# A second level of seven products for the graph layer's weights, and the residual and both biases added by accumulating DMAs

## The chip, the cores and the metric

The kernel runs on one NeuronCore of a Trainium2 chip. The metric is the device time in microseconds of one execution, the median of three runs. Profiles come from a separate profiled execution, whose own time is given beside its span.

## The reference

Two graph layers on x of shape 32 x 512 x 512 (batch, node, feature) in fp32, with one 512 x 512 adjacency matrix. Cut to what matters:

```
q, k, v = x @ Wq + bq, x @ Wk + bk, x @ Wv + bv            # 8 heads of 64
weights = softmax(q k^T / 8 + (adj == 0 ? -1e9 : 0))       # over the neighbours j
x1      = layernorm(x + weights @ v)                        # per node, over 512 features
deg     = adj.sum(1);  A = adj * deg^-1/2 (rows) * deg^-1/2 (columns)
out     = layernorm(x1 + A @ (x1 @ W1) + b1)
```

Each row of the softmax weights sums to one, so the bias of v may be added to the attention's output instead of to v.

## The kernel before

Everything is done per batch element, in fp32, and the engines overlap the work of several batches. `stretch` (two heads pairs at a time, `ORDER[:2]` and then `ORDER[2:]`) computes the scores, masks them on VectorE, takes the exponential on ScalarE, sums the numerators on GpSimd (`accumulate`), and multiplies by v. A batch b has two stretches. Between the first and the second stand the key and query projections of batch b + 1; after the second stand, in one list of pieces that `play` walks through, the convolution of batch b - 1 and the values of batch b + 1. The text calls this last list the second half of b. TensorE therefore repeats: scores and value products, projections, scores and value products, second half.

Projections are not plain products. Both 512-long dimensions are cut in two, and `seven` forms the four blocks of a result from seven products instead of eight, with sums of input blocks prepared beforehand (`combine` for x, `weigh_part` for weights; slots 4 to 6 hold sums, slot 2 is overwritten). A table such as `CHAIN` lists for each product its PSUM region (A, B, D), the two slots, and where its running sum goes: `put` writes a block, `add` adds to one. A region keeps accumulating over its products, so the next product on a region has to wait until the last one's running sum has been read out. The values of batches 1 and up use a second level: the four products of `CHAIN` that the table `OUTER` doesn't list are themselves one 2 x 2 block product, and `LEAF` does it by seven products of quarter size (four matmuls of 128 x 128 by 128 columns each) with quarter sums of x (`quarter`, `QUARTERS`) and of Wv (`weigh_quarters`, `wv_quarters`). A half-size product is four matmuls with 256 columns. One matmul in fp32 stands in the trace as two records.

The convolution of batch b - 1 comes in two factors. The first (`first`) multiplies the normalised x1, split in a high and a low part (`hi`, `lo`), by the transposed adjacency, and ScalarE copies the result into a tile `zT`. The second (`second`) multiplies it by W1 with the seven half-size products of `CHAIN`; each running sum goes through `move` on VectorE, and `put` adds x1 with b1 (in `yT`) on the way, so that the tile `y` holds the sum. After that come statistics, normalisation and the store.

What sets the order: TensorE, VectorE, ScalarE and GpSimd run in the order in which the program calls them (`InOrder`); `play(main, beside)` walks through `main`, which calls TensorE, and after piece n calls what `beside[n]` lists for the other engines. Waits between engines are semaphores, put in by the framework from the tiles' uses. Transfers issued on SyncE may be placed by the scheduler. [...]

Lines the change touches, by their function: the bias of v is added on GpSimd by `bias_values`, four adds of 128 x 512 per batch; the residual x is loaded by `load_residual` into a tile `xr` (four transfers of 256 KB on SyncE) and added to `yT` on GpSimd by `add` in `finish`; b1 is added on GpSimd by `lift`. `yT` is the attention's output after a transposition by VectorE and DMAs of 128-byte runs (`unload_values`), scaled by the softmax's inverse sums on VectorE (`scale`). `NUM` is a tile of eight numerators of 128 x 1024, taken in rotation by `numerators()`; each stretch takes exactly eight. `load_x` loads the next x in two halves, one into a tile of its own, the other into slot 7 of `NUM`. `wqv` holds either the query or the value weights; `swap` reloads it from DRAM twice a batch.

Of the kernel before, what the change touches and what calls it, by code (L numbers as in the profile page):

```python
# [18 lines left out]
P = 128  # L19
# [31 lines left out]
def unshifted(  # L51
# [61 lines left out]
    X = {}  # L113
# [9 lines left out]
    def load_x(b, j):  # L123
        if j == 1:
            X[b, j] = NUM[:, 7].rearrange("p k (n t r) -> p (k n) t r", t=DT, r=32)
        else:
            X[b, j] = acts.tile([P, 8, DT, 32], F32, name="x", bufs=1)
        for q in range(4):
            nc.sync.dma_start(
                X[b, j][32 * q : 32 * (q + 1)],  # L130
                x[b, ts(j, HALF), ts(q, P)].rearrange("(k s) (t r) -> s k t r", s=32, r=32),
            )
# [51 lines left out]
    def load_residual(b):  # L184
        if b < LAST - 1:
            t = acts.tile([P, NT, D], F32, name="xr", tag="zT", bufs=1)
        else:
            t = wk[:, 3:].rearrange("p k u o -> p k (u o)")
        R[b] = [t[:, i, :] for i in range(NT)]
        for i in range(NT):  # L190
            nc.sync.dma_start(R[b][i], x[b, ts(i, P), :])

# [33 lines left out]
    R[0] = acts.tile([P, NT, D], F32, name="xr", tag="zT", bufs=1)  # L226
    R[0] = [R[0][:, i, :] for i in range(NT)]

    wv = NUM[:, :4].rearrange("p e k (u o) -> p (e k) u o", u=2)
    for i in range(2):  # L230
        for k, engine in enumerate((nc.sync, nc.scalar)):
            engine.dma_start(R[0][2 * i + k], x[0, ts(2 * i + k, P), :])
            load_parts(Wv, "wv", engine, wv, [(i, 2 * k), (i, 2 * k + 1)])
        if i == 0:
            bv_r = load_row(bv, "bv_r", nc.scalar)
# [14 lines left out]
    stored = [drams.tile([P, 7, 2, HALF], F32, name=f"{name}_parts") for name in ("wq", "wv")]  # L250

    def weigh_quarters(engine):
        old, new = wv[:, 1:5].rearrange("p k u (r o) -> p k u r o", r=2), wv_quarters
        engine.tensor_tensor(new[:, 0], old[:, :, 0, 1], old[:, :, 1, 1], ALU.add)
        engine.tensor_tensor(new[:, 1], new[:, 0], old[:, :, 0, 0], ALU.subtract)
        engine.tensor_tensor(new[:, 2], old[:, :, 0, 0], old[:, :, 0, 1], ALU.subtract)
        engine.tensor_tensor(old[:, :, 0, 1], old[:, :, 1, 0], new[:, 1], ALU.subtract)
# [49 lines left out]
    def degrees():  # L307
# [37 lines left out]
    LEAF = tuple(CHAIN[k] for k in (0, 1, 3, 2, 5, 4, 6))  # L345
    OUTER = (
        ("A", (0, 0), (("add", (0, 0)),)),
# [4 lines left out]
    def seven(table, multiply, put, add, shape=(2, HALF)):  # L352
        regions = {}

        def step(region, ij, moves):
            fresh = region not in regions
            if fresh:
                regions[region] = bank([P, *shape])
            p = regions[region]
            multiply(p, *ij, fresh)  # L360
            for kind, q in moves:
                (put if kind == "put" else add)(q, p)

        return each(step, *table)
# [7 lines left out]
    def values_of(b):  # L372
# [10 lines left out]
        def multiply_quarters(p, i, j, fresh):  # L383
            for n, (k, l) in enumerate(((1, 1), (3, 2), (2, 3), (4, 4))):
                right = w[:, k, i % 2, ts(i // 2, P)] if i < 4 else wv_quarters[:, i - 4, k - 1]
                left = XT[:, l, j % 2, ts(j // 2, P)] if j in (0, 1, 3) else QUARTERS[:, max(j - 3, 0), l - 1]
                tensor.matmul(p[:, n, :], left, right, start=fresh and n == 0, stop=True, skip_group_check=True)

        def quarter_of(r, t):
            v = V[b].rearrange("p (j t) (i r o) -> p t r j i o", t=2, i=2, r=2)  # L390
            return v[:, t, r]

        def put_quarters(q, p):
            out(0, 0)
            scalar.copy(quarter_of(*q), p.rearrange("p (j i) o -> p j i o", i=2))

        def add_quarters(q, p):
            to = quarter_of(*q)
            vector.tensor_add(to, to, p.rearrange("p (j i) o -> p j i o", i=2))

        def spread_last():
            gpsimd.tensor_add(out(0, 1), out(0, 1), out(1, 1))

# [13 lines left out]
        leaf = seven(LEAF, multiply_quarters, put_quarters, add_quarters, (4, P))  # L417
        return leaf + [spread_last] + seven(OUTER, multiply, put, add)

    def bias_values(b, n, engine=gpsimd):  # L420
        engine.tensor_add(V[b][:, n, :], V[b][:, n, :], bv_r)
# [152 lines left out]
    def finish(b):  # L574
# [95 lines left out]
        def grow(i):  # L670
# [3 lines left out]
        all_, behind = range(NT), (NT - 1, *range(NT - 1))  # L674
        return dict(
            sums0=[lambda: sums(b, 0, bank([P, N]))], inverse0=[lambda: inverse(0, bank([P, N]))],
# [11 lines left out]
    def convolve(b):  # L688
        t = {}
        last = b == LAST  # L690
# [18 lines left out]
        def take(d, p, copy):  # L709
            if d == 0:  # L710
                t["z"] = XT[:, :4] if last else acts.tile([P, 4, 2, HALF], F32, name="zT", bufs=1)
# [7 lines left out]
        def combine(at):  # L719
            if at == 0:  # L720
                if last:
                    t["parts"] = XT[:, 4:]
                elif b == LAST - 2:
                    t["parts"] = wk[:, :3]
                else:
                    t["parts"] = acts.tile([P, 3, 2, HALF], F32, name="parts", tag="hi", bufs=1)
            to, a, c = PARTS[at]
            engine = vector if last and at < 2 else gpsimd
            engine.tensor_tensor(slot(to), slot(a), slot(c), ALU.subtract)

# [5 lines left out]

        def multiply(p, i, j, fresh):
            if "y" not in t:
                if last:
                    t["y"] = [numerators() for _ in range(2)]  # L740
                else:
                    if b == LAST - 2:
                        y = XT[:, 7:].rearrange("p k u o -> p k (u o)")
                    else:
                        y = acts.tile([P, NT, D], F32, name="y", tag="lo", bufs=1)
                    t["y"] = [y[:, 2 * k : 2 * k + 2, :] for k in range(2)]
# [7 lines left out]
        aside, extend = b == LAST - 1, []  # L754

# [34 lines left out]
        def store(n, at):  # L790
# [12 lines left out]
            parts=each(combine, *range(4)),  # L803
# [24 lines left out]
    weigh_quarters(gpsimd)  # L828
    nc.sync.dma_start(stored[1], NUM[:, :4].rearrange("p e k (u o) -> p (e k) u o", u=2)[:, :7])
    nc.sync.dma_start(stored[0], wqv)  # L830
    run(each(bias_values, *((0, n) for n in range(NT))))
# [6 lines left out]
    quarters()  # L838
# [4 lines left out]
    for b in range(B):  # L843
# [3 lines left out]
        if 1 < b < LAST:  # L847
            load_residual(b - 1)
        if b + 2 < B:
            load_x(b + 2, 0)  # L850
        if b == LAST:
            load_residual(b)
        stretch(b, one, back["measure"][:3] if back else ())
# [12 lines left out]
        if b < LAST:  # L866
            k0, k1 = keys_and_queries(b + 1, 0), keys_and_queries(b + 1, 1)
            main = [p for pair in zip(k0, k1) for p in pair]
            if b == 0:
# [4 lines left out]
                    7: weights[2:3], 8: exact[2:3], 9: weights[3:], 10: exact[3:],  # L874
                }
            else:
# [3 lines left out]
                    0: rest + scale + ahead["add"], 1: store[:1] + fold0, 2: store[1:2], 3: store[2:3] + fold1,  # L880
                    4: store[3:] + measure[:2], 5: measure[2:] + ahead["root"] + [quarters], 7: norm[:1] + ahead["judge"],
                    8: norm[1:2] + low[:1], 9: norm[2:3] + low[1:2], 10: norm[3:] + low[2:3],
                    11: low[3:] + ahead["lift"],
                }
            play(main, beside)
        else:
# [5 lines left out]
                3: conv["parts"][1:] + e["inverse0"] + ahead["grow"],  # L892
            })

        if b < LAST:
            swap(1)
        stretch(b, two, f[b]["pairs"][0] + f[b]["pairs"][1] if b == LAST else ())
# [3 lines left out]
        if b + 2 < B:  # L901
            load_x(b + 2, 1)
        if b < LAST:
            end = f[b]
            v, bias_v = values_of(b + 1), each(bias_values, *((b + 1, n) for n in range(NT)))
            back_to_queries = [lambda: swap(0)] if b < LAST - 1 else []
            if b == 0:
                play(v, {
                    1: fold0, 5: fold1, 8: turn0, 9: turn1 + combined[:2], 10: bias_v + combined[2:] + back_to_queries,
                })  # L910
            else:
                conv = c[b - 1]
                second = conv["second"]
                k = 6 if b < LAST - 1 else 8
                main = conv["first"] + v[:k] + second[:1] + v[k:9] + second[1:2] + v[9:10] + second[2:3] + v[10:] + second[3:]
                grow, parts, scale = ahead["grow"], conv["parts"], end["scale"]
                if b < LAST - 1:
                    beside = {
                        1: parts[:1] + fold0, 3: parts[1:], 5: fold1, 6: grow[:1], 7: end["inverse"], 8: grow[1:2],
                        9: grow[2:3] + scale[:1], 10: grow[3:] + scale[1:2], 11: scale[2:3], 13: turn0, 14: scale[3:],  # L920
                        15: turn1 + combined[:2], 17: combined[2:] + back_to_queries + bias_v,
                    }
                else:
                    measure, norm, low = end["measure"], end["norm"], end["low"]
                    beside = {
                        0: [lambda: load_residual(LAST - 1)], 1: parts[:1] + fold0, 3: parts[1:], 5: fold1,
                        6: grow[:1], 7: end["inverse"], 8: grow[1:2] + scale[3:], 9: grow[2:3] + scale[:1], 10: grow[3:] + scale[1:3] + end["add"],
                        14: measure[:2], 15: measure[2:3], 16: measure[3:] + end["root"],
                        17: norm[:1] + bias_v, 18: norm[1:2] + low[:1], 19: norm[2:3] + low[1:2],
                        20: norm[3:] + low[2:3], 21: low[3:] + end["lift"],  # L930
# [314 lines left out]
```

## Time and profile before

| | |
|---|---|
| median of three runs | 2732.93 us (2732.28 to 2732.99) |
| profiled execution, its own time | 2731.85 us |
| its span | 2730.0 us |
| granted TensorE clock | 0.998 |
| one batch, from TensorE's timeline | 83.78 us |
| of it, the second half from its first value product | 23.84 us |

The page's names are those of tiles with numbers left out: `w` is W1's tile (`w1`), `e` is `NUM`, `mm`, `sc` and `av` are PSUM tiles, `v`, `y`, `yT`, `zT`, `parts` and `xT` are as in the code. Nearly every instruction has line 45, that of `InOrder`, so groups are told apart by tiles. A timeline line gives start, length, engine, operation, output and inputs, how many instructions were merged, and in brackets the idle time before it with what ended it.

### The profile page before, as it was taken

To read this page: it belongs to the slowest core of one execution; us is meant where nothing else is said; L and a number is where in the kernel's file an instruction comes from. 1 tells how busy PE (TensorE), PEld (TensorE's weight loads), DVE (VectorE), ACT (ScalarE), POOL (GpSimd) and SP (SyncE) were. 2 spreads that over 40 slices of the span, in tenths; PEclk is the share of its full clock that TensorE was granted. 3 is DMA by queue.
4 is the path that set the end of the run, shared out by engine and by line. 5 is a ranking of instruction groups with operands and counts; after the bars stand their busy time and mean duration, and the time that the engine had idled before them with its cause. 6 is when DMAs were issued, how large, how long until landed. Compare 5 with 4: busy or idle time off the path is not lost.

```text
span 2730.0 us, 36290 instructions
## 1 busy us (share of the span) xinstructions
PE 2700.8 (99%) x13284; PEld 1907.7 (70%) x13284; DVE 2023.7 (74%) x2809; ACT 1260.5 (46%) x1807; POOL 2026.7 (74%) x1335
## 2 busy tenths in 40 slices
PE   9999999999999999999999999999999999999997
PEld 6676676766767767767667677677676676766765
DVE  4777776777777778767777777777777776777777
ACT  3335444454444454444544445444445444454444
POOL 5778777778777787777777777877778777778775
PEclk9999999999999999999999999999999999999999
DMA  6222333323333233333232332333333333323321
GB/s 181 86 74 88 101 89 99 107 69 105 93 105 97 76 103 104 89 97 97 82 104 86 103 106 73 101 107 90 94 90 92 101 89 98 107 70 104 98 61 45
DMA packets 388186, 256.75 MB, mean 94 GB/s; under 512 B 278816, under 2 KB 346400, under 8 KB 379936
## 3 DMA queue, kind: packets, MB, share of 16 engines
q1 hardware_dynamic: 386848, 252.78, 30.8%
q8 instruction: 107, 1.75, 0.3%
q10 hardware_dynamic: 1152, 1.57, 0.2%
q14 instruction: 79, 0.65, 0.1%
HBM read 183.77 MB, written 37.22 MB: 81 GB/s over the span
## 4 chain that ended last, share of the span: by engine, by line
PE 97%; DVE 2%; ACT 0%; DMA 0%; issue 0%; POOL 0%; SPq 0%; POOLq 0%; DVEq 0%; ACTq 0%
PE mm L45 64%; PE sc L45 17%; PE av L45 16%; DVE st L45 0%; DVE yT L45 0%; DVE xT L45 0%; DVE lo L45 0%; DVE v L45 0%; DVE kq L45 0%; POOL y L45 0%; DMA xr<-in_x_dram 0%; SPq L509 0%; DVE e L45 0%; DVE mv L45 0%; DVE folded L45 0%
## 5 line engine op out<-in xcount | busy, mean ns | idle before, releaser
L45 ACT ACTIVATE e<-e 128x1024 f32<-128x1024 f32 x512 | 541.3, 1057 | 598.1 <-DVE e L45 565.2
L45 DVE SCALAR_TENSOR_TENSOR e<-sc,maskT 128x1024 f32<-128x1024 f32 x512 | 584.9, 1214 | 99.4 <-PE sc L45 99.4
L45 POOL TENSOR_TENSOR acc<-acc,e 128x1024 f32<-128x1024 f32 x248 | 589.1, 2376 | 19.5
L45 POOL TENSOR_TENSOR xT<-xT 128x512 f32<-128x512 f32 x250 | 342.8, 1385 | 176.4 <-DVE xT L45 168.9
L45 PE MATMUL mm<-xT,wk 128*128 128x256 f32 x1792 | 463.4, 381 | 2.3 <-DVE kq L45 2.3
L45 PE MATMUL mm<-xT,wqv 128*128 128x256 f32 x1792 | 459.9, 379 | 0.0
L45 PE MATMUL sc<-kq 64*128 64x512 f32 x2048 | 458.7, 596 | 0.2 <-DVE kq L45 0.2
L45 PE MATMUL av<-e,v 128*64 128x512 f32 x2048 | 453.6, 595 | 0.3
L45 POOL TENSOR_TENSOR acc<-e 128x1024 f32<-128x1024 f32 x126 | 297.5, 2362 | 133.7 <-ACT e L45 133.7
L45 PEld LDWEIGHTS mm<-xT,wk 128*128 128x128 f32 x1792 | 337.4, 190 | 72.7 <-DVE mv L45 23.5
L45 PEld LDWEIGHTS mm<-xT,wqv 128*128 128x128 f32 x1792 | 340.5, 190 | 46.3
L45 PEld LDWEIGHTS av<-e,v 128*64 128x64 f32 x2048 | 146.5, 137 | 300.1 <-issue 242.1
L45 PEld LDWEIGHTS sc<-kq 64*128 64x128 f32 x2048 | 191.7, 186 | 235.3 <-issue 181.6
L45 ACT ACTIVATE kq<-mm,bias 128x256 f32<-128x256 f32 x512 | 214.5, 473 | 288.2 <-PE mm L45 285.5
L45 PE MATMUL mm<-wqv,xT 128*128 128x128 f32 x1736 | 302.2, 320 | 4.5 <-DVE v L45 4.5
L45 PEld LDWEIGHTS mm<-wqv,xT 128*128 128x128 f32 x1736 | 261.6, 191 | 27.8 <-issue 3.9
L45 DVE STREAM_TRANSPOSE yb<-av 128x512 f32<-128x512 f32 x127 | 91.0, 717 | 253.3 <-DMA yT<-yb 197.6
L45 DVE TENSOR_TENSOR v<-v,mm 128x512 f32<-128x512 f32 x221 | 146.2, 685 | 149.9 <-PE mm L45 148.9
L45 PE MATMUL mm<-w,zT 128*128 128x256 f32 x992 | 229.7, 379 | 0.2 <-DVE xT L45 0.2
L45 POOL TENSOR_TENSOR yT<-yT,b_r 128x512 f32<-128x512 f32 x126 | 156.9, 1277 | 64.3 <-DVE lo L45 64.3
L45 PEld LDWEIGHTS mm<-w,zT 128*128 128x128 f32 x992 | 186.0, 190 | 25.3 <-issue 1.4
L45 PE MATMUL mm<-adjT,hi 128*128 128x512 f32 x512 | 201.6, 397 | 0.7 <-ACT e L45 0.7
(133 smaller groups left out, 3465.1 us busy)
## 6 DMA issues: line engine op xcount, KB each, us to landing
wqv<-wv_parts SPq DMA_DIRECT2D x31, 1792.0 KB, 7.6
wqv<-wq_parts SPq DMA_DIRECT2D x30, 1792.0 KB, 7.0
yT<-yb SPq DMA_DIRECT2D x508, 64.0 KB, 2.4
out_dram<-y SPq DMA_DIRECT2D x120, 256.0 KB, 2.0
xr<-in_x_dram SPq DMA_DIRECT2D x118, 256.0 KB, 3.4
x<-in_x_dram SPq DMA_DIRECT2D x124, 128.0 KB, 2.7
e<-in_x_dram SPq DMA_DIRECT2D x124, 128.0 KB, 2.6
wk<-in_x_dram SPq DMA_DIRECT2D x8, 256.0 KB, 2.7
```

The costliest lines, as they stand in the source:

```text
L45: return self.tc.keep_in_program_order(op(*args, **kwargs))
```

## The change

- The second factor of the convolution, for batches 0 to 29, uses the second level too: `LEAF` on quarters of z and of W1 (`quarter` inside `convolve`, `w1_quarters`), then `spread_last` and `OUTER`. Its leaf's `put` is a copy on ScalarE; x1 with b1 is added afterwards to `y` by GpSimd (`combined`, listed as `join`, four adds), placed before the running sums of the last two outer products.
- `LEAF` gets another order of its seven products, for the values as well, and `OUTER`'s first product is split in two: the matmuls, and later the add.
- The residual, bv and b1 are added to `yT` by DMAs with accumulation, issued on GpSimd's queue (`gather`; `rows` repeats a bias row): one of x and one of bv in the second half, one of b1 at the end of the projections. In batches 0, 30 and 31 the residual is still loaded and added, with bv added to it by such a DMA. `bias_values` goes.
- z, its sums and its quarters lie in slots 0 to 4 of `NUM`; the first half of the next x is loaded into slot 6, after the second stretch. The tiles `zT` and `parts` remain for batch 30, `x` and most of `xr` go.
- W1 with its sums is also stored to DRAM and loaded again after batch 30's second half, since its quarter sums overwrite a part of it.
- In the second half TensorE's order becomes: first factor, values' leaf, the convolution's first outer product, the values' first, the convolution's leaf, and then the outer products of the two in turn. Batch 30's `low` moves to the last batch's first stretch.

The core of the diff:

```diff
     def load_x(b, j):
-        if j == 1:
-            X[b, j] = NUM[:, 7].rearrange("p k (n t r) -> p (k n) t r", t=DT, r=32)
-        else:
-            X[b, j] = acts.tile([P, 8, DT, 32], F32, name="x", bufs=1)
+        X[b, j] = NUM[:, 6 + j].rearrange("p k (n t r) -> p (k n) t r", t=DT, r=32)
...
+    def gather(to, source):
+        gpsimd.dma_start(to, source, accum_op=ALU.add)
+
+    def rows(v):
+        return bass.AP(tensor=v.tensor, offset=v.offset, ap=[[0, P], [0, NT], [1, D]])
...
-    LEAF = tuple(CHAIN[k] for k in (0, 1, 3, 2, 5, 4, 6))
+    LEAF = tuple(CHAIN[k] for k in (0, 1, 2, 5, 4, 3, 6))
     OUTER = (
-        ("A", (0, 0), (("add", (0, 0)),)),
+        ("A", (0, 0), ()),
+        ("A", None, (("add", (0, 0)),)),
         ("A", (5, 5), (("add", (0, 1)),)),
         ("A", (6, 6), (("add", (1, 1)), ("add", (1, 0)))),
     )
...
+    def quarters_of(left, w, w_quarters, target, begin):
+        def multiply(p, i, j, fresh):
+            for n, (k, l) in enumerate(((1, 1), (3, 2), (2, 3), (4, 4))):
+                right = w[:, k, i % 2, ts(i // 2, P)] if i < 4 else w_quarters[:, i - 4, k - 1]
+                tensor.matmul(p[:, n, :], left(j, l), right, start=fresh and n == 0, stop=True, skip_group_check=True)
+
+        def to(r, t):
+            begin()
+            return target().rearrange("p (j t) (i r o) -> p t r j i o", t=2, i=2, r=2)[:, t, r]
+
+        def put(q, p):
+            scalar.copy(to(*q), p.rearrange("p (j i) o -> p j i o", i=2))
+
+        def add(q, p):
+            vector.tensor_add(to(*q), to(*q), p.rearrange("p (j i) o -> p j i o", i=2))
+
+        return seven(LEAF, multiply, put, add, (4, P))
...
+        def combined(i, j):
+            gpsimd.tensor_add(of(t["y"], i, j), of(t["y"], i, j), old(i, j))
+
+        def spread_last():
+            gpsimd.tensor_add(of(t["y"], 0, 1), of(t["y"], 0, 1), of(t["y"], 1, 1))
...
-                main = conv["first"] + v[:k] + second[:1] + v[k:9] + second[1:2] + v[9:10] + second[2:3] + v[10:] + second[3:]
+                main = (
+                    conv["first"] + main + other[:1] + [lambda: run(outer[:2])] + conv["leaf"] + other[1:2]
+                    + [conv["spread_last"]] + outer[2:3] + other[2:3] + outer[3:] + other[3:]
+                )
...
                 if b < LAST - 1:
                     beside = {
-                        1: parts[:1] + fold0, 3: parts[1:], 5: fold1, 6: grow[:1], 7: end["inverse"], 8: grow[1:2],
-                        9: grow[2:3] + scale[:1], 10: grow[3:] + scale[1:2], 11: scale[2:3], 13: turn0, 14: scale[3:],
-                        15: turn1 + combined[:2], 17: combined[2:] + back_to_queries + bias_v,
+                        1: parts[:1] + fold0, 3: parts[1:] + fold1, 5: end["inverse"], 9: scale[:1], 10: scale[1:3],
+                        12: scale[3:] + grow, 13: turn0 + turn1 + end["residual"] + combined[:1], 22: join[:1], 23: join[1:2],
+                        24: join[2:3] + combined[1:2], 25: join[3:] + combined[2:], 26: end["residual_bias"] + [lambda: swap(0)],
                     }
```

Where the text speaks of an x-combination it means `combined` of `turns`, the sums of the next x's blocks.

## The prediction

> **What bounds the kernel now.** I read the page's busy shares and chain first, then the busy time of one batch by stage, then the timelines of TensorE, VectorE and GpSimd in that batch (1013 to 1097 us, typical: the chain repeats every 83.78 us).
>
> ```profile
> PE 2700.8 (99%) x13284; PEld 1907.7 (70%) x13284; DVE 2023.7 (74%) x2809; ACT 1260.5 (46%) x1807; POOL 2026.7 (74%) x1335
> PE 97%; DVE 2%; ACT 0%; DMA 0%; issue 0%; POOL 0%; SPq 0%; POOLq 0%; DVEq 0%; ACTq 0%
> ...
> 1020.58:1044.42 23.84, 23.84 (x140) 21.49 (x138) 14.75 (x25) 5.39 (x9) 14.62 (x12) 1.00 0.40 123
> ```
>
> TensorE is the bound nearly everywhere, at full clock. The window line is the stage that the change rebuilds (columns: length, then PE, PEld, DVE, ACT, POOL busy): TensorE fills all 23.84 us.
>
> ```profile
> 1020.58 1.05 PE L45 MATMUL mm<-wqv,xT 128*128 128x128 f32 x8
> 1021.47 1.06 PE L45 MATMUL mm<-wv_quarters,xT 128*128 128x128 f32 x8
> ...
> 1037.42 1.89 PE L45 MATMUL mm<-w,zT 128*128 128x256 f32 x8
> 1039.14 1.89 PE L45 MATMUL mm<-w,parts 128*128 128x256 f32 x8
> ...
> 1044.42 7.14 PE L45 MATMUL sc<-kq 64*128 64x512 f32 x32
> 1051.49 7.09 PE L45 MATMUL av<-e,v 128*64 128x512 f32 x32
> ```
>
> That is TensorE's timeline in the same stage and after it. Start to start, a quarter product (four matmuls, eight records) takes 0.893 us and a half-size product 1.727 us. Records start every 0.112 and 0.216 us.
>
> ```profile
> 106.64 0.97 PEld L45 LDWEIGHTS mm<-wv_quarters,xT 128*128 128x128 f32 x8
> 107.53 0.97 PEld L45 LDWEIGHTS mm<-wqv,xT 128*128 128x128 f32 x8
> 107.84 0.59 ACT L45 COPY v<-mm 128x512 f32<-128x512 f32 x1 [1.20 <-PE mm L45]
> 108.54 0.97 PEld L45 LDWEIGHTS mm<-wv_quarters,xT 128*128 128x128 f32 x8
> 108.87 1.87 DVE L45 TENSOR_TENSOR v<-v,mm 128x512 f32<-128x512 f32 x3
> 110.86 0.19 PEld L45 LDWEIGHTS mm<-wqv,xT 128*128 128x128 f32 x1 [1.35 <-issue]
> ```
>
> The timeline of all engines around 108 us shows the one leaf that today runs without other products between, batch 0's. The product loaded at 106.64 is copied out by ScalarE at 107.84, 0.31 after its last matmul starts (106.75 + 7 x 0.112). The next product on that bank, one product later, loads at 108.54 where the cadence gives 107.53 + 0.893 = 108.42: a stall of **0.12**. VectorE's adds end at 110.74 and the load they release is at 110.86, again 0.12 later.
>
> ```profile
> 1041.38 4.95 POOL L45 TENSOR_TENSOR v<-v,bv_r 128x512 f32<-128x512 f32 x4
> ...
> 1044.53 0.69 DVE L45 TENSOR_TENSOR y<-yT,mm 128x512 f32<-128x512 f32 x1 [1.04 <-PE mm L45]
> 1045.59 9.14 DVE L45 SCALAR_TENSOR_TENSOR e<-sc,maskT 128x1024 f32<-128x1024 f32 x8 [0.38 <-PE sc L45]
> ...
> 1051.48 0.20 PEld L45 LDWEIGHTS av<-e,v 128*64 128x64 f32 x4 [0.76 <-POOL acc L45]
> ```
>
> These are GpSimd's, VectorE's and the weight loads' timelines at the stage's end. GpSimd starts independent 128x512 adds every 1.23 us, 1.27 each; the dependent pair in the parts starts 1.35 apart (1020.67, 1022.02). The score masks start 1.17 after the scores and follow every 1.13. The fifth ends at 1045.59 + 4 x 1.13 + 1.22 = 1051.33, and the weight load of the value products follows 0.15 later. The built order makes that load wait for the fifth mask. So **any delay of the first mask moves TensorE one for one**.
>
> **What the Trainium skill says.** "SBUF — State Buffer", Who interferes with whom: a VectorE instruction with two SBUF inputs contends with a GpSimd instruction that reads SBUF, one with at most one doesn't. The trace agrees: the b1 adds take 1.27 at the median and 1.735 at most, the long ones beside VectorE's `lo`. "Perfetto Trace Analysis", Matmuls: groups should rotate through banks so that evacuation overlaps; the 0.12 above is what returning early costs here. "DMA: Bandwidth & Descriptors", SWDGE vs HWDGE vs iDMA: accumulation during a DMA is GpSimd's alone, whose cores write the descriptors. No row of before shows one.
>
> **The change, part by part.** It acts on 30 second halves (batches 1 to 30, with the convolutions of 0 to 29).
>
> *Matmuls.* Out: four half-size products, 4 x 1.727 = 6.91. In: seven quarter products, 7 x 0.893 = 6.25. **-0.66**, times 30 = -19.7 us.
>
> *Leaf order.* Both leaves now run A(0,0), D(4,4), A(5,5), D(2,3), A(6,6), B(1,1), A(3,2), with nothing between but the row-sum matmul (0.22, after D(4,4), in V's leaf alone). Returning to A after one product costs 0.12: at A(6,6) in V's leaf (A(5,5) is covered by the row-sum matmul), at A(5,5) and A(6,6) in the convolution's. D(2,3) has a stall before it or that matmul, so nothing. A(3,2) waits for VectorE's add from A(6,6): last load + 0.11 to its matmul + 0.31 + 0.68 + 0.12 = 1.22, against nine starts, 1.01: 0.21 each. V's leaf 0.33, the convolution's 0.44: **+0.77**. The saving is already spent.
>
> *Tail.* Let L be the start of the first half-size product after the convolution's leaf; four follow, and scores start at S = L + 6.91. ScalarE's copy of A(3,2) ends at L + 0.78. GpSimd waits for it, then does in order: spread, join (0,1), join (1,1), join (0,0), an x-combination, join (1,0). Starts: 0.86, +1.35, then four times +1.23 = L + 7.11; the last ends at L + 8.38. VectorE's last y add waits for that join, and the masks stand behind it: add L + 8.44 to 9.13, first mask at about S + 2.14 instead of S + 1.17. **+0.97**, paid at the fifth mask. Bounds: 0.15 if GpSimd were never late (two y adds instead of one follow the last product), and 2.4 if the six operations took 1.5 each, the mean of today's spread (1518 ns in its group). VectorE reads PSUM in all its adds there, so I take 1.27.
>
> *Accumulating DMAs.* Three per stage, 1 MB each, on GpSimd's queue. Issue: the page above gives about 1 us to the first byte (Latency and other measured facts); bounds nothing and 6 us (512 rows of 2 KB). I take 1 to 2. The residual one stands after V's spread (about 1032.5; it waits for VectorE's scaling, done by 1030) and before the x-combination (1.35) and the convolution's spread at L + 0.86 = 1038.4: up to 4.2 us is free. The bias one delays the accumulations from about S + 5.6 to S + 4.05 + issue; VectorE wants their last fold at S + 22.4 and they take 14.5, so up to 3.8 is free. The b1 one has the start of the next scores as cover. Landing: 6.15 us for 1 MB (Bandwidth), 12.3 if the second read doubles it (estimate); the residual has 15 us before GpSimd waits for it, the bias some 16 before the statistics, b1 over 30. Nothing.
>
> *GpSimd's removed adds* (bias 4 x 1.29, residual 4 x 1.28, b1 4 x 1.28) gain nothing: nobody on the path waited for them. *Four quarter subtractions* (5.1) end by 1031.5; the last is needed at A(3,2), about 1036. Four puts go from VectorE to ScalarE (2.4; it is 46% busy). *First x half* into slot 6: its load waits for the accumulation of that slot, lands by 1025, turned at 1031.8. The query parts are reloaded after V's last product, about 1042.8 instead of 1037.61; they land in 7.0 and are wanted at 1059. Residual loads leave SP (1.8 us, hidden). Batch 0's leaf loses about 1 of its 2.9 us of VectorE stalls; batch 30's `lo` (4 x 1.0) moves into the last batch, where the convolution may wait 1. Zero together.
>
> **Sum:** -0.66 + 0.77 + 0.97 = +1.08 a stage, +32.4 us. Against the profiled execution's 2731.85 (span 2730.0) that is 2764; the median 2732.93 stands 1.1 above it, so **2765 us**.
>
> **Rivals.** *The matmul saving survives* (faster): the weight loads after A(6,6) and A(5,5) find their banks free, because evacuation runs ahead of the latencies measured at 108 us, and GpSimd's chain from spread to join ends before S + 0.5. Price -0.66 x 30: 2713. It decides when leaf and tail waits together fall under 0.66 a stage. Against it: the 0.12 is measured, and six operations cannot start closer than 1.23. *Leaf stalls only*: the join is in time, tail 0.15: (-0.66 + 0.77 + 0.15) x 30 = +8, 2741; with slightly smaller stalls within 0.2% of before. For it: GpSimd spans are rough. *Descriptor writing or landing is slow*: every microsecond of issue over 4.2 delays spread and join; 6 us gives 1.8 x 30 = 54 more, 2819. For it: no row shows such a DMA; against it: the page's 1 us. *That leaf products don't save* is excluded by the 0.893.
>
> **Numbers.** Sized as computed 0.65 (2752 to 2778), saving survives 0.07, leaf stalls only 0.14, slow descriptors 0.14. 0.2% of 2733, 5.5 us, is about what a measurement can tell from no change. Faster 0.08, same 0.07, slower 0.85. The range 2738 to 2795 drops the full saving, the low half of "leaf stalls only" and the upper part of slow descriptors.
>
> **What would show it.** TensorE's timeline: quarter products of `w` at 0.893 spacing with gaps of 0.1 to 0.2 before A(6,6) and A(3,2). VectorE's last y add waiting for POOL y, the first mask some 2.1 after the scores start, the value products at S + 8.0 instead of S + 7.07. Wrong if the join ends before the last product, or if GpSimd idles little before the convolution's spread.

## The result and the profile after

The changed kernel takes 2805.4 us (median of six runs, 2803.86 to 2805.72), the kernel before 2732.96 beside it: a ratio of 1.0264, 95% interval 1.0251 to 1.0277. That is 72.4 us slower, where 32 were forecast; the time lies outside the range of 2738 to 2795. The span of the profiled execution grew from 2730.0 to 2803.7.

The page's busy shares and chain of the changed kernel, and the busy time by stage (length, then PE, PEld, DVE, ACT, POOL busy):

```profile
PE 2731.0 (97%) x14004; PEld 1929.7 (69%) x14004; DVE 2130.2 (76%) x2809; ACT 1329.1 (47%) x1927; POOL 2062.0 (74%) x1336
PE 89%; DVE 8%; issue 2%; POOL 0%; DMA 0%; ACT 0%; SPq 0%; DVEq 0%; POOLq 0%; ACTq 0%
...
1039.52:1064.75 25.23, 23.96 (x164) 22.02 (x162) 18.14 (x24) 7.73 (x13) 19.91 (x15) 1.00 0.44 83
```

VectorE's share of the chain went from 2% to 8%. The window is the rebuilt stage: it grew from 23.84 to 25.23 us although it has fewer matmuls, and TensorE is idle for 1.27 of it. VectorE's busy time there rose from 14.75 to 18.14 for about as many instructions (25 and 24).

TensorE's timeline in that stage and after it:

```profile
1039.52 1.05 PE L45 MATMUL mm<-wqv,xT 128*128 128x128 f32 x8
...
1044.32 2.16 PE L45 MATMUL mm<-wqv,xT 128*128 128x128 f32 x16
1046.32 1.89 PE L45 MATMUL mm<-w,e 128*128 128x256 f32 x8
...
1054.45 1.06 PE L45 MATMUL mm<-w,e 128*128 128x128 f32 x8
1056.78 1.13 PE L45 MATMUL mm<-w,e 128*128 128x128 f32 x8 [1.27 <-DVE y L45]
1057.74 1.89 PE L45 MATMUL mm<-wqv,xT 128*128 128x256 f32 x8
...
1064.75 7.82 PE L45 MATMUL sc<-kq 64*128 64x512 f32 x32
1072.66 7.09 PE L45 MATMUL av<-e,v 128*64 128x512 f32 x32
```

The value leaf (1039.52 to 1046.32) is as forecast: its last two products, from 1044.32 on, take 2.00 instead of 1.79. The convolution's leaf is not. Between the start of its B(1,1) at 1054.45 and that of its A(3,2) at 1056.78 lie 2.33 us, a quarter product (0.893) and **1.44** of waiting; the forecast had 0.21 there. (The 1.27 in the line's brackets is less, because a line's length runs past the start of the next product.) To compare kernels below, the text takes the time from the start of B(1,1) to the start of the product behind A(3,2): 3.29 us here, 1.79 for two quarter products without a wait. The value products start 7.91 after the scores, 7.07 before.

From the first adjacency product of one second half to that of the next is 86.03 us on average over 29 batches (171.80 to 2666.70), against 83.78 before: **+2.25 a batch**, 65.4 of the 73.6 us of span. The start is 3.6 faster (up to the end of batch 1's second stretch), and batch 30's second half with the last batch 11.9 slower.

The chain of waits through that stage, in order of time (start, length, what):

```profile
1049.22 0.87 DVE yT L45
...
1050.83 1.76 DVE yT L45
1052.58 0.60 DVE v L45
1053.18 0.50 DVE xT L45
...
1054.27 1.20 DVE xT L45
1055.46 1.18 DVE y L45 x2
1056.64 0.14 issue
1056.78 8.04 PE mm L45 x40
```

It enters VectorE's queue well before the wait: scaling (`yT`), the value leaf's outer add (`v`), the two turns of the next x (`xT`), and only then the two y adds, the second of which A(3,2) waits for. VectorE's and GpSimd's timelines in the changed kernel say why it is late:

```profile
1045.41 0.69 DVE L45 TENSOR_TENSOR v<-v,mm 128x512 f32<-128x512 f32 x1 [0.21 <-PE mm L45]
1046.02 6.57 DVE L45 TENSOR_TENSOR yT<-yT,inv 128x512 f32<-128x512 f32 x4
1052.51 0.67 DVE L45 TENSOR_TENSOR v<-v,mm 128x512 f32<-128x512 f32 x1
1053.11 2.36 DVE L45 STREAM_TRANSPOSE xT<-e 128x1024 f32<-128x1024 f32 x2
1055.39 1.84 DVE L45 TENSOR_TENSOR y<-y,mm 128x512 f32<-128x512 f32 x3
...
1040.45 9.91 POOL L45 TENSOR_TENSOR e<-e 128x512 f32<-128x512 f32 x7 [1.89 <-ACT e L45]
1050.32 1.71 POOL L45 TENSOR_TENSOR v<-v 128x512 f32<-128x512 f32 x1
```

Four scalings take 6.57 us, and nearly all that time GpSimd is on SBUF operations of its own: the last three of the four new quarter subtractions (the 9.91 us are three sums of z and these four), and the spread. The same four, in the tile's statistics (minimum, median, maximum in ns) of the kernel before:

```profile
L45 DVE TENSOR_TENSOR yT<-yT,inv x124: 672/684/2834, 138.6 to 2621.4; 128x512 f32<-128x512 f32 x124
```

and of the changed kernel:

```profile
L45 DVE TENSOR_TENSOR yT<-yT,inv x124: 678/1755/1789, 137.9 to 2687.1; 128x512 f32<-128x512 f32 x124
```

The median scaling went from 0.68 to 1.76 us.

At the end of the stage, VectorE's last y add waits for GpSimd's last join and the masks stand behind it, as forecast:

```profile
1066.17 0.69 DVE L45 TENSOR_TENSOR y<-y,mm 128x512 f32<-128x512 f32 x1 [0.56 <-POOL y L45]
1066.77 9.14 DVE L45 SCALAR_TENSOR_TENSOR e<-sc,maskT 128x1024 f32<-128x1024 f32 x8
```

The first mask starts 2.02 after the scores, 1.17 before.

On the scaling, the page that the prediction cites, "SBUF — State Buffer" of the Trainium skill, section Who interferes with whom, names this pair: VectorE with two SBUF inputs (`yT` and `inv`) beside a GpSimd instruction that reads SBUF. The trace agrees, with 0.68 and 1.76 as above.

### The profile page after: what moved, and what is told of

Its sections match the earlier page's. It is cut to its first block, busy times and chain, and to the rows that moved or that the text cites. A ratio compares the mean times of both kernels' runs of the same rounds, so it can differ in the third digit from the quotient of the medians.

```text
span 2803.7 us, 38312 instructions
## 1 busy us (share of the span) xinstructions
PE 2731.0 (97%) x14004; PEld 1929.7 (69%) x14004; DVE 2130.2 (76%) x2809; ACT 1329.1 (47%) x1927; POOL 2062.0 (74%) x1336
## 4 chain that ended last, share of the span: by engine, by line
PE 89%; DVE 8%; issue 2%; POOL 0%; DMA 0%; ACT 0%; SPq 0%; DVEq 0%; POOLq 0%; ACTq 0%
PE mm L45 56%; PE sc L45 17%; PE av L45 16%; DVE yT L45 3%; DVE xT L45 2%; DVE y L45 1%; DVE v L45 1%; DMA yT<-yb 0%; DVE st L45 0%; DVE lo L45 0%; POOL yT L45 0%; DVE yb L45 0%; DMA xr<-in_x_dram 0%; ACT xT L45 0%; SPq L507 0%
## 5 line engine op out<-in xcount | busy, mean ns | idle before, releaser
L45 PE MATMUL sc<-kq 64*128 64x512 f32 x2048 | 478.7, 605 | 0.5 <-ACT zT L45 0.4
L45 POOL TENSOR_TENSOR e<-e 128x512 f32<-128x512 f32 x244 | 331.6, 1370 | 75.5 <-ACT e L45 57.3
L45 PEld LDWEIGHTS sc<-kq 64*128 64x128 f32 x2048 | 184.7, 186 | 262.6 <-issue 142.0
L45 PEld LDWEIGHTS av<-e,v 128*64 128x64 f32 x2048 | 158.3, 137 | 299.8 <-issue 223.9
L45 PE MATMUL mm<-w,e 128*128 128x128 f32 (+1 forms) x1680 | 299.1, 321 | 37.3 <-DVE y L45 36.8
L45 PE MATMUL mm<-wqv,xT 128*128 128x128 f32 x1736 | 309.4, 322 | 2.5 <-DVE v L45 2.4
L45 PEld LDWEIGHTS mm<-w,e 128*128 128x128 f32 x1680 | 252.8, 191 | 61.6 <-issue 41.5
L45 POOL TENSOR_TENSOR rstd<-ve,minus_half 128x4 f32<-128x4 f32 (+1 forms) x66 | 66.1, 1002 | 233.7 <-DVE nmu L45 230.8
## 6 DMA issues: line engine op xcount, KB each, us to landing
wqv<-wv_parts SPq DMA_DIRECT2D x31, 1792.0 KB, 11.9
yT<-in_L_gnn_bias_dram POOLq DMA_DIRECT2D x30, 1024.0 KB, 14.5
```

Source lines behind the costliest of these rows:

```text
L45: return self.tc.keep_in_program_order(op(*args, **kwargs))
```

## The experiments

The theory after this reading: (1) the convolution leaf's wait is VectorE's lateness, made of slow scaling and of the turns queued before the adds; (2) the tail is GpSimd's chain, as forecast; (3) the DMAs cost nothing; (4) the last batch has a loss of its own. Rivals: DMAs are behind it, only one half of (1) is, or VectorE is short everywhere so that nothing helps.

The batch time below is always the average over those 29 batches. Where two of these kernels differ by less than about 6 us, their intervals overlap, and what is said of them rests on the traces.

| kernel | time, us | ratio to before (interval) | batch, us |
|---|---|---|---|
| before | 2731 to 2733 | | 83.78 |
| changed | 2805.4 | 1.0264 (1.0251 to 1.0277) | 86.03 |
| no quarter subtractions | 2761.2 | 1.0107 (1.0091 to 1.0124) | 84.53 |
| joins first | 2784.8 | 1.0194 (1.0177 to 1.0211) | 85.37 |
| turns after the leaf | 2779.1 | 1.0177 (1.016 to 1.0194) | 85.14 |
| no accumulating DMAs | 2801.3 | 1.0253 (1.0236 to 1.027) | 86.01 |
| grow late | 2800.6 | 1.0254 (1.0237 to 1.0271) | 86.03 |
| turns split | 2750.2 | 1.0069 (1.0052 to 1.0086) | 84.24 |
| leaves apart | 2776.2 | 1.0168 (1.0151 to 1.0185) | 84.95 |
| scale early | 2777.4 | 1.0168 (1.0151 to 1.0185) | 84.96 |
| last join early | 2749.1 | 1.0063 (1.0051 to 1.0075) | 84.24 |
| all repairs | 2750.1 | 1.0067 (1.0055 to 1.0079) | 84.24 |
| turns behind | 2729.2 | 0.9991 (0.9985 to 0.9998) | 83.71 |

**No quarter subtractions.**

```diff
-                parts = conv["parts"] + conv["quarters"]
+                parts = conv["parts"]
```

> Leaves out the convolution's four quarter subtractions on GpSimd in the second halves (the leaf multiplies what lies in those places), so that GpSimd is not beside VectorE's scaling for most of it. Theory (VectorE is late for the convolution leaf's A(6,6) add because the four scalings take 1.66 us each beside GpSimd's subtractions instead of 0.73 alone): scaling falls to 1.2 us or less at the mean, TensorE's wait before A(3,2) from 1.27 to under 0.3, time 2769 us (36 less than the changed kernel). Rival (the two turns queued ahead of the adds are cause enough, 2.36 us): scaling may fall, but the wait stays above 0.9 and the time above 2795. Rival (the accumulating DMAs): 2805, no change.

VectorE's and TensorE's timelines of this kernel in one stage:

```profile
1030.89 3.60 DVE L45 TENSOR_TENSOR yT<-yT,inv 128x512 f32<-128x512 f32 x4
...
1039.21 2.10 PE L45 MATMUL mm<-w,e 128*128 128x128 f32 x16
1041.15 1.89 PE L45 MATMUL mm<-wqv,xT 128*128 128x256 f32 x8
```

Scaling takes 3.60 us instead of 6.57; the one slow scaling left (1.79) is the one beside the spread. From B(1,1) to the product behind A(3,2) it is 1.94 us instead of 3.29, so of the wait 0.15 is left, with both turns where they were. The batch falls by 1.50 and the time by 44 us, 8 more than expected; the tail is unchanged at 7.92. The new GpSimd work cost TensorE this wait without touching TensorE: through the speed of VectorE.

**Joins first.**

```diff
-                        24: join[2:3] + combined[1:2], 25: join[3:] + combined[2:],
+                        24: join[2:3], 25: join[3:] + combined[1:],
```

> Only moves one x-combination of the tail behind the last join on GpSimd. Theory (the tail's 0.84 us a stage is GpSimd's chain of six operations from the leaf's spread to the last join): the last join ends 1.23 earlier, VectorE's last y add and the first mask come in time, value products start some 7.2 instead of 7.9 after the scores, time 2785 us (0.7 x 28 = 20 less). Rival (the scores are late for another reason, VectorE's queue or the slower weights reload): value products stay at 7.9, time 2805.

Value products start 7.27 after the scores and the batch falls by 0.67: 2784.8, as expected. One GpSimd instruction of 1.27 us ahead of the last join was three quarters of the tail.

**Turns after the leaf.**

```diff
-                        12: scale[3:] + grow, 13: turn0 + turn1 + end["residual"] + combined[:1], 22: join[:1], 23: join[1:2],
-                        24: join[2:3] + combined[1:2], 25: join[3:] + combined[2:], 26: end["residual_bias"] + [lambda: swap(0)],
+                        12: scale[3:] + grow, 13: end["residual"], 20: turn0 + turn1, 22: join[:1], 23: join[1:2],
+                        24: join[2:3], 25: join[3:] + combined, 26: end["residual_bias"] + [lambda: swap(0)],
```

> Moves both turns of the next x on VectorE from before the convolution's leaf to behind its A(3,2), and with them all four x-combinations behind the last join. Theory (VectorE's queue of scaling, value add and both turns makes the A(6,6) add late): the wait before A(3,2) falls from 1.27 to under 0.3 even with scaling at 1.66, and the tail is repaired as in the kernel with the joins first, time 2751 us (1.2 + 0.7 a stage, 28 stages). Rival (the slow scaling alone makes it late, the turns are hidden): the wait stays above 0.9 and the time is that of the joins alone, 2785.

TensorE's and VectorE's timelines of this kernel:

```profile
1045.24 2.16 PE L45 MATMUL mm<-w,e 128*128 128x128 f32 x16
1047.24 1.89 PE L45 MATMUL mm<-wqv,xT 128*128 128x256 f32 x8
1049.93 1.99 PE L45 MATMUL mm<-w,e 128*128 128x256 f32 x8 [0.80 <-DVE y L45]
...
1046.94 2.36 DVE L45 STREAM_TRANSPOSE xT<-e 128x1024 f32<-128x1024 f32 x2
1049.23 0.65 DVE L45 TENSOR_TENSOR y<-y,mm 128x512 f32<-128x512 f32 x1
```

Neither expectation. From B(1,1) to the product behind A(3,2) it is 2.00 us, 0.21 more than two products, with the scaling as slow as in the changed kernel (a median of 1.75): so the turns were needed for the wait. But the pair now stands in front of the y add after the leaf, and the product that reuses that bank starts 2.69 after the one before it instead of 1.73. Of 1.3 us gained, 0.96 is paid two products later: the forecast of 2751 missed by 28 us.

**No accumulating DMAs.**

```diff
-            residual=[residual], residual_bias=[lambda: gather(YT[b], rows(bv))],
-            lift_all=[lambda: gather(YT[b], rows(b1))],
+            residual=[], residual_bias=[],
+            lift_all=[],
```

> Leaves out residual, value bias and b1 of the batches that get them by accumulating DMA (three DMAs of 1 MB a batch), all else as in the changed kernel. Theory (these DMAs lie off the path, as forecast): wait before A(3,2) and tail stay, time 2800 to 2806 us. Rival (writing their descriptors, 1.3 us each on GpSimd, or their landings of 9 to 14 us, cost the path): 1 us a stage or more comes back, time under 2775.

As the theory has it: batch 86.01 against 86.03, and before A(3,2) the trace still has 1.27 of idle time, as in the changed kernel. The DMAs are not behind the loss.

**Grow late** (the last batch alone).

```diff
-                3: conv["parts"][1:] + e["inverse0"] + ahead["lift"] + ahead["grow"],
+                3: conv["parts"][1:] + e["inverse0"] + ahead["lift"],
...
-        stretch(b, two, f[b]["pairs"][0] + f[b]["pairs"][1] if b == LAST else ())
+        stretch(b, two, f[b]["pairs"][0] + f[b]["pairs"][1] + ahead["grow"] if b == LAST else ())
```

> Only the last batch: ScalarE's four scalings of batch 30's rows by rdeg, which wait for GpSimd's b1 adds, move behind the last scores' eight exponentials. Theory (in the changed kernel they stand in front of these exponentials on ScalarE and hold back the last value products, 4.9 us late at their start and 2.6 more at their end): 7 us less than the changed kernel, 2798 us. Rival (the last exponentials are late for the masks or the matmuls): 2804 to 2806.

ScalarE's timeline of the changed kernel in the last batch shows what is moved:

```profile
2736.40 0.72 ACT L45 ACTIVATE yT<-yT,rdeg 128x512 f32<-128x512 f32 x1 [5.26 <-POOL yT L45]
...
2740.10 0.72 ACT L45 ACTIVATE yT<-yT,rdeg 128x512 f32<-128x512 f32 x1 [0.51 <-POOL yT L45]
2740.72 7.66 ACT L45 ACTIVATE e<-e 128x1024 f32<-128x1024 f32 x8
```

The last eight exponentials queue behind four scalings that wait for GpSimd's b1 adds. The scalings stood there before as well, but the adds were done by then: the last one started at 2644 us, the scalings at 2663. Moved behind, the last value products start 4.4 us sooner after their scores and end 2.6 sooner still. Part is paid again: GpSimd's last sums of numerators then run beside VectorE's residual adds (16 of these take 10.1 us instead of 6.2), and a row-sum product waits 1.2 for GpSimd. The span falls by 5.1 of the 7 expected, the median (ratio 1.0254 for 1.0264) by about 3, which the overlapping intervals don't tell apart from nothing: the order of waits is shown by the trace, the gain in time is not.

**Turns split.** The joins first and the grow late as above, and

```diff
-                        12: scale[3:] + grow, 13: turn0 + turn1 + end["residual"] + combined[:1], 22: join[:1], 23: join[1:2],
-                        24: join[2:3] + combined[1:2], 25: join[3:] + combined[2:], 26: end["residual_bias"] + [lambda: swap(0)],
+                        12: scale[3:] + grow, 13: turn0 + end["residual"], 22: turn1 + join[:1], 23: join[1:2],
+                        24: join[2:3], 25: join[3:] + combined, 26: end["residual_bias"] + [lambda: swap(0)],
```

> Joins ahead of all x-combinations, ScalarE's order in the last batch as in the kernel with the grow late, and the two turns apart: the first where it is, the second behind the y add that follows the leaf. Theory (VectorE's queue before the A(6,6) add and before the y add after the leaf is too long by about one turn each): both waits under 0.35, time 2744 us (20 for the joins, 7 for the end, 1.2 x 28 = 34 for the wait less than the changed kernel). Rival (VectorE is short in the whole stage, so a turn moved anywhere is paid later, as 0.8 of 1.3 was with both turns moved): waits of 0.5 or more remain, 2765 or more.

TensorE's timeline of this kernel:

```profile
1037.38 2.31 PE L45 MATMUL mm<-w,e 128*128 128x128 f32 x16
1039.52 1.89 PE L45 MATMUL mm<-wqv,xT 128*128 128x256 f32 x8
```

From B(1,1) to the product behind A(3,2) it is 2.14 us: 0.35 of the wait is left, and the wait after the leaf is gone. The batch falls by 1.13 below the joins-first kernel, and the time is 2750, 6 above the expectation. So taking away the slow scaling removes nearly all of the wait, and taking away one of two turns, with the scaling still at 1.75, removes most of it. VectorE was 1.4 us late in the changed kernel (its add of A(6,6) starts at 1055.96; 0.31 after that product's last matmul would be 1054.58). The slow scaling was worth 3.0 of VectorE's time (6.57 to 3.60), a turn 1.2.

**Leaves apart** and **scale early.** B(1,1) earlier in both leaves, a half-size product of the other side ahead of each A(3,2); in the second also an earlier inverse and first scaling.

```diff
-    LEAF = tuple(CHAIN[k] for k in (0, 1, 2, 5, 4, 3, 6))
+    LEAF = tuple(CHAIN[k] for k in (0, 1, 3, 2, 5, 4, 6))
...
+                    conv["first"] + leaf[:6] + other[:1] + leaf[6:] + [spread_last]
+                    + conv["leaf"][:6] + [lambda: run(outer[:2])] + conv["leaf"][6:] + other[1:2]
```

> As the kernel with the turns split, with the leaves' products taken apart: B(1,1) earlier, one half-size product of the other side before each leaf's A(3,2). Theory (what is left of the leaf stalls, 0.33 in the value leaf and 0.5 in the convolution's, comes from returning to a bank after one product): about 0.6 a stage less than with the turns split, 2727 us, faster than the kernel before. Rival (VectorE's scaling then ends too late for the leaf, which starts 2 us earlier): no gain, 2744 or more.

> As the kernel with the leaves apart, with the row-sum matmul and the inverse one product earlier and the first of the four scalings directly behind it on VectorE, in an idle stretch. Theory (VectorE is 1.5 us earlier at the convolution's leaf): the same time as with the leaves apart if no wait for VectorE was left there, 2727 us, and up to 10 us less if one was. Rival (the yb transfers have not landed by then, so the scaling waits and holds the value adds): slower by 5 us or more.

They took 2776.2 and 2777.4 us. The first is on its rival's side (2744 or more), though not for the rival's reason; the second can't be told from the first, so its own rival (5 us slower) is out. In both, the first turn overwrites slot 0 of `xT` ahead of the moved value product that reads it, so that product multiplies the next x. Whatever it multiplies, ScalarE's and TensorE's timelines of the first of them show a wait that neither theory nor rival had named:

```profile
1042.83 2.56 ACT L45 ACTIVATE yT<-yT,rdeg 128x512 f32<-128x512 f32 x4
1045.29 1.05 ACT L45 COPY y<-mm 128x512 f32<-128x512 f32 x2
...
1046.00 1.13 PE L45 MATMUL mm<-w_quarters,e 128*128 128x128 f32 x8 [1.01 <-ACT y L45]
```

The leaf starts 2 us earlier, and its first two copies stand behind ScalarE's four scalings by `rdeg`. The first two batches also lost some 5 us, with the other leaf order (see the last kernel). The earlier scaling made no difference that can be seen (84.96 and 84.95 a batch).

**Last join early** (in the turns-split kernel).

```diff
-                        24: join[2:3], 25: join[3:] + combined,
+                        24: join[3:], 25: join[2:3] + combined,
```

> As the kernel with the turns split, and the last two joins exchanged: join (1,0), for which VectorE's last y add waits, ahead of join (0,0), for which nobody on the path waits. Theory (the rest of the tail, value products 7.27 after the scores against 7.07 before, is that join): 7.07, 0.2 x 28 = 5.6 us less than the turns split, 2745 us; what is left over the kernel before is the leaves' own stalls. Rival (VectorE's own queue sets the first mask): 7.27 stays, 2750.

The rival was right: 7.27 stays. In VectorE's timeline two y adds follow the last product, 1.28 us together, and the masks begin behind them; before, one did.

**All repairs.** The turns split, the last joins exchanged, the leaves apart, `grow` before the leaf's copies, the turn of slots 2 and 3 in front of the leaf and that of slots 0 and 1 behind it, and batch 30's b1 by a DMA.

> The repairs together: as the kernel with the last joins exchanged, with the leaves' products taken apart (B(1,1) earlier, one half-size product ahead of each A(3,2)), ScalarE's scalings by rdeg ahead of the leaf's copies, the turn into the slots that no later product reads in the place before the leaf and the other behind it, and batch 30's b1 by an accumulating DMA too. Theory (returning to a bank after one or no product costs 0.9 a stage, of which the order takes back half): 0.45 x 28 = 13 less than the kernel with the joins exchanged, and 3 to 5 at the end, 2728 us, a little faster than before. Rival (the leaf, now 2 us earlier, waits for VectorE's slow scaling): 2745 or more.

2750.1 us, as the rival had it: the gain of the order is paid again. In TensorE's timeline A(3,2) waits for VectorE's y add (0.62 us counted from start to start), since the leaf is earlier and the scaling is not:

```profile
1042.95 1.13 PE L45 MATMUL mm<-w,e 128*128 128x128 f32 x8 [0.46 <-DVE y L45]
```

The first two batches are 5.5 slower.

**Turns behind.** As all repairs, with

```diff
-                        12: scale[3:], 13: turn1 + end["residual"], 22: turn0 + join[:1], 23: join[1:2],
-                        24: join[3:], 25: join[2:3] + combined,
+                        12: scale[3:], 13: end["residual"], 22: turn0 + join[:1], 23: join[1:2],
+                        24: turn1 + join[3:], 25: join[2:3] + combined,
```

and, beside these lines, batch 0's leaf in the changed kernel's order and batch 30's b1 DMA one piece later.

> As the kernel with all repairs, with both turns behind the leaf (one after the y add that follows it, one after the next y add, where VectorE idles), batch 0's leaf in the changed kernel's order and batch 30's b1 DMA behind the statistics' roots. Theory (the 0.46 wait before A(3,2) in the kernel with all repairs is VectorE, which the turn in front of the leaf makes late; the first batch lost 5.5 by the other order): a stage costs 83.78 again as before, the first batch 171.5 at its end, time 2730 us: the saved matmuls (0.66 a stage) are then just used up by what the leaves' waits (0.4) and the first mask (0.2) cost. Rival (the turns are then paid at the masks): a stage at 84.2 as with the joins exchanged, 2744.

TensorE's timeline of this kernel:

```profile
1028.88 1.13 PE L45 MATMUL mm<-w_quarters,e 128*128 128x128 f32 x8
1029.85 1.89 PE L45 MATMUL mm<-wqv,xT 128*128 128x256 f32 x8
1031.58 1.05 PE L45 MATMUL mm<-w,e 128*128 128x128 f32 x8
1032.52 1.99 PE L45 MATMUL mm<-wqv,xT 128*128 128x256 f32 x8
...
1039.62 7.17 PE L45 MATMUL sc<-kq 64*128 64x512 f32 x32
1046.89 7.09 PE L45 MATMUL av<-e,v 128*64 128x512 f32 x32
```

A(3,2) at 1031.58 follows its neighbour without a gap. The stage takes 23.55 us (1016.07 to 1039.62): 23.18, which is the 23.84 of before less the 0.66 of saved products, and 0.37 of small waits. The batch costs 83.71, 0.07 less than before, and the time is 2729.2, as expected: 0.09% under the kernel before (0.02 to 0.15), less than the prediction held to be measurable. Of 0.66 us of saved products a batch, the leaves' waits keep 0.37 and the second y add 0.20. The start is back too: the first adjacency product of the second half of batch 1 stands at 171.49, against 177.05 with all repairs, and up to there batch 0's leaf is what differs between the two.

## Why the prediction was right and wrong

Right in sign (0.85 for slower) and in most steps; the size was off by 41 of 73 us of span, for two reasons: the convolution's leaf and the last batches.

- *Matmuls, -0.66 a stage*: consistent; with it and 0.37 of small waits, all seen in TensorE's timeline, the stage of the last kernel comes out.
- *Value leaf, +0.33*: measured 0.32 (1039.52 to 1046.32, less 7 x 0.893 and the row sum's 0.23).
- *Convolution leaf, +0.44*: **this step failed**, at its term "A(3,2) waits for VectorE's add from A(6,6) ... 0.21 each". That assumed that VectorE is free when the last matmul of A(6,6) ends. It was 1.4 us late, and the term measured 1.44; the leaf cost 1.72 in all (1049.77 to 1057.74, less 7 x 0.893). The cause stands in another sentence of the prediction, priced at nothing: "Four quarter subtractions (5.1) end by 1031.5". They ended when forecast (10.8 us after the first value product), but they ran beside the scaling, which the change had also moved into one block, and made three of the four about 1 us slower each (the fourth is slow beside the spread). The prediction had cited the rule of interference and applied it to the length of GpSimd's own adds, not to VectorE, the other partner. The two turns, which the change puts side by side in front of the y adds, are the other part: without either part, most of the wait is gone.
- *What the kernel before already showed.* The long b1 adds (1.735 at most) do not run beside `lo`, as the prediction reads them, but beside VectorE's own b1 adds in the last batch, which have two SBUF inputs. And the price of the scaling could be read. In batch 1 of the kernel before, it ran as one block beside GpSimd's sums of numerators; in the changed kernel GpSimd is idle for most of it. First before, then changed:

```profile
138.62 6.65 DVE L45 TENSOR_TENSOR yT<-yT,inv 128x512 f32<-128x512 f32 x4
...
137.92 3.50 DVE L45 TENSOR_TENSOR yT<-yT,inv 128x512 f32<-128x512 f32 x4
```

- *Tail, +0.97*: measured 0.84, by the mechanism named: 0.64 went with the x-combination alone. The lower bound of 0.15, "two y adds instead of one follow the last product", was the remaining 0.20.
- *Accumulating DMAs, nothing*: right in cost. An issue occupies GpSimd for 1.3 us (1 to 2 assumed); the landings took 9.2 to 14.5 us at the median (6.15 to 12.3 assumed), and the batch was the same without these DMAs (86.01 and 86.03). The rival with slow descriptors, which lay nearer to the measured time (2819), is excluded by the kernel without these DMAs.
- *Batches 0, 30 and 31, "Zero together"*: the start gained 3.6 (1 was forecast, from batch 0's leaf). That leaf gave 0.5; most of the rest is a wait of TensorE for VectorE's copies into `kq`, 2.3 us at 157.10 in the kernel before and gone in the changed one. The shorter scaling block of batch 1, above, would explain it, but that was not tested: the 2.6 beyond the forecast were luck. From batch 30's second half on, 11.9 were lost where about 2 were forecast: the prediction priced the wait for `lo` alone and missed that batch 30's `lift`, now late too, holds back `grow`, which stands in front of the last exponentials on ScalarE. Moving them changed the end of the last value products by 7 us, counted from the scores. The other losses there, among them `lo` beside GpSimd's sums, were not taken apart.

Sum: 29 x (2.25 - 1.08) = 34 from the stages, 10 at the end, less 2.6 at the start: the 41. Two sums of the prediction are off in the second decimal (0.12 + 0.12 + 0.21 is 0.45, and the tail's starts add up to L + 7.13), which changes nothing.

Still open is how the 1.4 us divide between scaling and turns: removing either one undoes most of the wait (0.15 is left without the slow scaling, 0.21 without both turns, 0.35 without one), so no division follows.

## What to carry to other kernels

Work given to GpSimd is not free merely because GpSimd has idle time: look for the two-input VectorE instructions that it will run beside, price them at the duration that the trace shows for the two side by side, and add up the whole VectorE queue in front of the next instruction that TensorE waits for. An operation taken out of the way of one wait has to be followed to the next reader behind it: the two turns, the exchanged products and the scalings by `rdeg` each came back as another wait. When a saving is 0.66 us in 84, every new instruction between the last product and the next stage (one more add, 0.20) is of its size.

## What the runs showed of the hardware

- A 128 x 512 VectorE multiply with two SBUF inputs takes 0.68 us alone and 1.76 beside GpSimd adds and subtractions (medians of the kernels before and changed); a GpSimd operation of the same size goes from 1.27 to between 1.60 and 1.72 in the same stretch.
- An accumulating DMA of 1 MB from DRAM into SBUF occupied GpSimd for 1.3 us and landed 9.2 to 14.5 us after its issue (medians). The weights' reload that starts beside one landed in 11.9 us instead of 7.6 (7.3 in the kernel without these DMAs), without a cost in time: the batch was the same with and without them. The changed kernel's DMA list (issues, KB each, median us to landing):

```profile
wqv<-wv_parts SPq DMA_DIRECT2D x31, 1792.0 KB, 11.9
...
yT<-in_L_gnn_bias_dram POOLq DMA_DIRECT2D x30, 1024.0 KB, 14.5
...
yT<-in_x_dram POOLq DMA_DIRECT2D x29, 1024.0 KB, 9.2
yT<-in_L_gnn_bv_dram POOLq DMA_DIRECT2D x29, 1024.0 KB, 9.5
```
